# Attention, then a quantized convolution block: weight quantization spread over nine query blocks, a band split ahead of the last sums, stores on two queues

## The chip, the cores and the metric

The kernel runs on one core of a Trainium2 chip. A core has a matrix engine (TensorE, PE in the profile), a vector engine (VectorE, DVE), an activation engine (ScalarE, ACT), a general one (GpSimd, POOL) and a queue engine (SyncE, SP); 16 DMA engines move data between the memory of the chip and that of the core. Each engine works its own list of instructions in order, and they wait for one another by semaphores. The metric is the device time of one execution in microseconds, the median of several runs.

## The reference

Layer 0 is group norm, attention with four heads over 4096 positions, and a residual. Layer 1 quantizes the weights of two 3x3 convolutions to three bits and runs convolution, batch norm, Relu, convolution, batch norm, residual, Relu. x is (4, 128, 64, 64) in float32.

```python
# layer 0
x_norm = _group_norm(x, norm_w, norm_b)
qkv = jnp.einsum('oc,bchw->bohw', qkv_w, x_norm) + qkv_b[None, :, None, None]
q, k, v = (to_heads(t) for t in jnp.split(qkv, 3, axis=1))      # (b, 4, 4096, 32)
attn = jax.nn.softmax(jnp.einsum('bhid,bhjd->bhij', q, k) * scale, axis=-1)
out = jnp.einsum('bhij,bhjd->bhid', attn, v)                    # back to (b, c, h, w)
x = x + jnp.einsum('oc,bchw->bohw', proj_w, out) + proj_b[None, :, None, None]
# layer 1; lsq_quantize: round(clip(w / alpha_s, -4, 3)) * alpha_s
residual = x
out = conv3x3_decomposed(x, lsq_quantize(w1, alpha1))
out = relu(batchnorm(out, gamma1, beta1))
out = conv3x3_decomposed(out, lsq_quantize(w2, alpha2))
out = relu(batchnorm(out, gamma2, beta2) + residual)
```

## The kernel before

**Attention.** A block is one image `b` and one of its eight chunks of 512 queries, `qb`; the 32 blocks run in the order of `blocks`, and I write (b,qb) for one. A block has 32 steps `kt`, one for each 128 keys. In a step, `scores` multiplies keys and queries for four heads on PE (L435) and ACT takes the exponential into a tile `p` (L437); one step later at least, `weights` multiplies `p` with the values into `acc` (L448). The sums over the keys are kept apart: in most steps DVE adds `p` to `r` (L460), one add of 128x2048, and in the six steps of `MOVED` an accumulating DMA, issued by POOL, adds `p` to `rm` instead (L453, L455). The tiles `p` come from a pool of eight.

PE's order is written out by hand: three pairs of scores, one step of weights, three pairs, two steps of weights, and so on (the while loop). After each step of weights, `side(kt)` runs what `schedule` has put at that place: a list of (step, function), sorted, made anew for each block. So a function's place in it sets the place of its instructions on every engine's list at once.

**What follows a block** runs inside the next one (`finish_parts`): `merge` adds `rm` to `r`, `sums` has PE reduce `r` over partitions (L477), then ACT evacuates `ls`, `spread`, `invert` and `gather` bring the reciprocals round by DMA (`lq`, `rd`, `rc`, on SP), `weigh` multiplies `av` by `rc` on DVE (L526) two steps ahead of `project` on PE (`po`, L310), and `store` adds bias and residual `x` on DVE (L536) and writes `y` by POOL's queue (L537). `weigh` stands at step 25 to 27, `project` at 27 to 29. In qb 1 to 7 of the first three images the projections of the next image run along as well.

**Quantization.** `quant_tasks` makes eight generators: for each of the two weights one for the scalars (nine tiny DVE instructions) and three for three taps each (a load of 128x384 on SP, L172, and 13 DVE instructions of 128x384, L174 to L189, with tiles `tk` and `tq` from the pool `stage`). `pieces` strings them together: each `next(pieces)` runs up to the next `yield`. Before the change the last four instructions of a group have no `yield` behind them and run together with the load of the next group. `schedule` takes six pieces a block at steps 1, 6, 11, 16, 21, 26 of the blocks (3,1) to (3,6); they are used up in (3,5).

**Convolution.** The output of attention is read back from `y` in bands of 16 rows (four an image, `bandlist`), with a zero border by POOL memsets (L549 to L555). `split` parts a band into `hi` and `lo` on DVE (L562, L563), and PE takes 18 matmuls for a half band (L752). The tiles of bands come from the nine buffers that held keys. The first two bands are loaded and split inside the last block, and their convolutions run ahead of and between the last block's sums and projection. These lines set the order there:

```python
    conv(ready[0, 0, 0], early[0][:, 1, :], 1, wq[0])
    last["sums_at_once"]()
    load_band(*bandlist[2])
    conv(ready[0, 0, 1], early[1][:, 0, :], 0, wq[0])
    conv(ready[0, 0, 1], early[1][:, 1, :], 1, wq[0])
    last["project"]()
    last["store"]()
    split_band(*bandlist[2])
    last["bounds"]()
```

`layer` then goes through the bands: statistics on DVE (L816), a copy by ACT (L817), with loads three bands and splits two bands ahead (`first`). At the very end, for each of 16 quarters of an image (the first in two halves), DVE scales and adds the residual (L912), ACT applies Relu (L913), and SP issues the store of 512 KB (L914).

Of the kernel before, what the change touches and what calls it, by code (L numbers as in the profile page):

```python
# [78 lines left out]
def _fast_body(ctx, tc, x, norm_w, norm_b, qkv_wt, qkv_b, proj_wt, proj_b,  # L79
               w1, alpha1, gamma1, beta1, w2, alpha2, gamma2, beta2, out, cnt):  # L80
    nc = tc.nc
    B, C, H, W = x.shape
# [3 lines left out]
    NB = N // FB  # L86
    NK = N // P
# [53 lines left out]
    def quant_tasks(pool):  # L141

        tasks = []
        for i, (w, alpha) in enumerate(((w1, alpha1), (w2, alpha2))):
            al = const.tile([P, 1], F32, name=f"al{i}")
            nc.gpsimd.dma_start(out=al, in_=alpha.partition_broadcast(P))
            t = {n: const.tile([P, 1], F32, name=f"{n}{i}")
                 for n in ("ag", "a_s", "a_c", "a_h", "a_l", "inv", "ninv")}
            alpha_s.append(t["a_s"])


            def scalars(al=al, t=t):
                nc.vector.tensor_scalar(t["ag"], al, gfac, None, ALU.mult)
                nc.vector.tensor_tensor(t["a_s"], al, t["ag"], ALU.subtract)
                nc.vector.tensor_tensor(t["a_s"], t["ag"], t["a_s"], ALU.add)
                nc.vector.tensor_scalar(t["a_c"], t["a_s"], 4097.0, None, ALU.mult)
                nc.vector.tensor_tensor(t["a_h"], t["a_c"], t["a_s"], ALU.subtract)
                nc.vector.tensor_tensor(t["a_h"], t["a_c"], t["a_h"], ALU.subtract)
                nc.vector.tensor_tensor(t["a_l"], t["a_s"], t["a_h"], ALU.subtract)
                nc.vector.reciprocal(t["inv"], t["a_s"])  # L160
                nc.vector.tensor_scalar(t["ninv"], t["inv"], -1.0, None, ALU.mult)
                yield

            tasks.append(scalars)
            for c in range(3):


                def taps(i=i, c=c, w=w, t=t):
                    tk, tq = (pool.tile([P, 2, FB], F32, name=f"t{n}{i}{c}", tag=n) for n in "kq")
                    wr, q0, qh, ql = (u[:, e, : 3 * P].rearrange("p (t o) -> p t o", o=P)  # L170
                                      for u in (tk, tq) for e in range(2))
                    nc.sync.dma_start(out=wr, in_=w[:, 3 * c : 3 * c + 3, :])  # L172
                    yield
                    nc.vector.tensor_scalar(q0, wr, t["inv"], -8.0, ALU.mult, ALU.max)  # L174
                    nc.vector.tensor_scalar(q0, q0, 8.0, None, ALU.min)
                    nc.vector.tensor_scalar(qh, q0, SPLIT, None, ALU.add)
                    yield
                    nc.vector.tensor_scalar(qh, qh, SPLIT, None, ALU.subtract)
                    nc.vector.tensor_tensor(ql, q0, qh, ALU.subtract)
                    nc.vector.scalar_tensor_tensor(wr, qh, t["a_h"], wr, ALU.mult, ALU.subtract)  # L180
                    yield
                    nc.vector.scalar_tensor_tensor(wr, qh, t["a_l"], wr, ALU.mult, ALU.add)
                    nc.vector.scalar_tensor_tensor(wr, ql, t["a_h"], wr, ALU.mult, ALU.add)
                    nc.vector.scalar_tensor_tensor(wr, ql, t["a_l"], wr, ALU.mult, ALU.add)
                    yield
                    nc.vector.scalar_tensor_tensor(q0, wr, t["ninv"], q0, ALU.mult, ALU.add)
                    nc.vector.tensor_scalar(q0, q0, QN, QP, ALU.max, ALU.min)
                    nc.vector.tensor_scalar(q0, q0, ROUND, None, ALU.add)
                    nc.vector.tensor_scalar(wq[i][:, 3 * c : 3 * c + 3, :], q0, ROUND, None,  # L189
                                            ALU.subtract)  # L190

                tasks.append(taps)
        return tasks
# [350 lines left out]
    def band_tile(name):  # L544
        return stack_tile(name).rearrange("p (r w) -> p r w", w=PW)

    def border(t, g):

        nc.gpsimd.memset(f32(t)[:, :, 0:1], 0.0)  # L549
        nc.gpsimd.memset(f32(t)[:, :, W + 1 : W + 2], 0.0)  # L550
        r0, r1 = g * BR - 1, g * BR + BR + 1
        if r0 < 0:
            nc.gpsimd.memset(f32(t)[:, 0, 1 : 1 + W], 0.0)
        if r1 > H:
            nc.gpsimd.memset(f32(t)[:, BR + 1, 1 : 1 + W], 0.0)  # L555
        lo, hi = max(r0, 0), min(r1, H)
        return f32(t)[:, lo - r0 : hi - r0, 1 : 1 + W], lo, hi

    def split(t, name):

        hi, lo = band_tile(f"hi{name}"), band_tile(f"lo{name}")
        nc.vector.tensor_copy(hi, f32(t))  # L562
        nc.vector.tensor_tensor(lo, f32(t), f32(hi), ALU.subtract)  # L563
        return hi, lo
# [3 lines left out]
    def load_band(b, g):  # L568
        raw[b, g] = t = band_tile(f"t0_{b}_{g}")
        inner, lo, hi = border(t, g)  # L570
        nc.sync.dma_start(out=inner, in_=y0[b].rearrange("p (h w) -> p h w", w=W)[:, lo:hi, :])

    def split_band(b, g):
        ready[0, b, g] = split(raw[b, g], f"0_{b}_{g}")
# [3 lines left out]
    for j in range(NB):  # L578
        eng = (nc.sync, nc.scalar)[j % 2]
# [21 lines left out]
    def load_kv(b, j):  # L601
        load_k(b, j)
        load_v(b, j)
# [18 lines left out]
    def schedule(n, before):  # L622
        b, qb = blocks[n]
# [5 lines left out]
        def add(kt, f):  # L629
            todo.append((kt, f))  # L630
# [7 lines left out]
        if before:  # L638
# [3 lines left out]
            kt = kts[-1]  # L642
# [50 lines left out]
                    add(4 * j + 1, lambda j=j: load_kv(b + 1, j))  # L693
        if b > 0 and qb == 0:
            add(1, lambda: load_kv(b, NB - 1))
        if b == B - 1 and 0 < qb < NB - 1:
            for kt in range(1, NK - 1, 5):
                add(kt, lambda: next(pieces, None))
        if n == len(blocks) - 1:
            add(5, lambda: load_band(0, 0))  # L700
            add(13, lambda: split_band(0, 0))
            add(17, lambda: load_band(0, 1))
            add(24, lambda: split_band(0, 1))
        return sorted(todo, key=lambda t: t[0])

    pieces = (piece for task in quant_tasks(stage) for piece in task())
    steps = len(blocks) * NK
    at = {"pair": 0, "step": 0}
# [11 lines left out]
    def run_weights(count):  # L720
        for _ in range(min(count, steps - at["step"])):
            n, kt = divmod(at["step"], NK)
            if kt == 0:
                assert not todo
                todo[:] = schedule(n, parts.get(n - 1))
            weights(at["step"])
            at["step"] += 1
            if kt == NK - 2:
                parts[n] = finish_parts(n)
            if kt == NK - 1:  # L730
                parts[n]["copy"]()
            else:
                side(kt)
# [9 lines left out]
    bandlist = [(b, g) for b in range(B) for g in range(H // BR)]  # L743

    def conv(parts, ps, j, w):
        hi, lo = parts
        r0 = j * RB
        n = 0
        for part in (hi, lo):
            for tap in range(TAPS):  # L750
                kh, kw = divmod(tap, 3)
                nc.tensor.matmul(ps.rearrange("p (r w) -> p r w", w=W), w[:, tap, :],  # L752
                                 part[:, r0 + kh : r0 + kh + RB, kw : kw + W],
                                 start=(n == 0), stop=(n == 2 * TAPS - 1))
                n += 1
# [7 lines left out]
    conv(ready[0, 0, 0], early[0][:, 0, :], 0, wq[0])  # L763
    last["residual"]()
    conv(ready[0, 0, 0], early[0][:, 1, :], 1, wq[0])
    last["sums_at_once"]()
    load_band(*bandlist[2])
    conv(ready[0, 0, 1], early[1][:, 0, :], 0, wq[0])
    conv(ready[0, 0, 1], early[1][:, 1, :], 1, wq[0])
    last["project"]()  # L770
    last["store"]()
    split_band(*bandlist[2])
    last["bounds"]()
    att.close()

# [130 lines left out]
    for b in range(B):  # L906
        for j in range(4):
            for p in range(2 if b == j == 0 else 1):
                n = HN // 2 if b == j == 0 else HN
                y = res[b, j][:, p * n : (p + 1) * n]  # L910
                cs = slice(j * HN + p * n, j * HN + (p + 1) * n)
                nc.vector.scalar_tensor_tensor(y, cv[b][:, cs], a2, y, ALU.mult, ALU.add)  # L912
                nc.scalar.activation(y, y, AF.Relu, bias=c2)  # L913
                nc.sync.dma_start(out=out[b].rearrange("c h w -> c (h w)")[:, cs], in_=y)  # L914

# [456 lines left out]
```

## Time and profile before

| | us |
|---|---|
| median of 5 runs | 2574.32 |
| lowest and highest | 2571.59, 2575.25 |
| the profiled execution | 2572.48 |
| its span, first to last instruction | 2570.7 |
| PE busy | 2525.8 (98%) |
| DVE busy | 2138.8 (83%) |
| ACT busy | 2083.3 (81%) |
| adds of `r`, L460 | 768 of 2.289 |
| exponentials, L437 | 2048 of 1.033 |
| stores of the output, first to last issue | 2543.79 to 2563.49 |

The clock granted to PE was 0.995 on average. Times within the execution count from the start of the span. A row of the profile names line, engine, operation and tile, and says what ended the idle time before it; idle time of an engine that nobody waits for costs nothing. Attention takes the span up to 2255.8, the first convolution up to about 2397, the second up to 2542.

### The profile page before, as it was taken

How to read it: one execution, taken by the hardware profiler on the slowest of the kernel's cores; microseconds unless marked ns; L12 is line 12 of the kernel's file. 1: busy time of each engine (PE TensorE's matmuls, PEld its weight loads, DVE VectorE, ACT ScalarE, POOL GpSimd, SP SyncE). 2: the span in 40 equal slices, each digit the busy share in tenths (PEclk: the TensorE clock that was granted, in tenths of full speed). 3: DMA queues.
4: the chain of work that ended last, by engine and by line, in shares of the span. 5: the costliest groups of instructions: out<-in, count | busy, mean ns of one | idle time of the engine just before them, and what ended most of it. 6: DMA issues, size and time to landing. Idle time of an engine off the chain costs nothing.

```text
span 2570.7 us, 48634 instructions
## 1 busy us (share of the span) xinstructions
PE 2525.8 (98%) x20504; PEld 1231.9 (48%) x20504; DVE 2138.8 (83%) x1401; ACT 2083.3 (81%) x2278; POOL 280.0 (11%) x459
## 2 busy tenths in 40 slices
PE   9999999999999999999999999999999999999995
PEld 5444444444444444444444444444444444467774
DVE  6898888889988889889988888888999998854344
ACT  5888899998989899998988899999889899911224
POOL 2111111111011111110011111110000001000000
PEclk9999999999999999999999999999999999999998
DMA  6876766688767667697766666986755756635004
GB/s 186 193 189 171 172 157 163 161 197 192 166 142 187 169 157 169 156 215 174 167 171 159 162 158 151 205 203 142 159 117 133 164 125 139 148 79 162 1 1 165
DMA packets 147562, 400.06 MB, mean 156 GB/s; under 512 B 59256, under 2 KB 60024, under 8 KB 118792
## 3 DMA queue, kind: packets, MB, share of 16 engines
q0 software_dynamic: 45792, 280.33, 48.4%
q1 hardware_dynamic: 100824, 115.10, 16.9%
q8 instruction: 163, 2.67, 0.4%
q10 hardware_dynamic: 720, 1.44, 0.2%
q14 instruction: 63, 0.52, 0.1%
HBM read 105.32 MB, written 55.83 MB: 63 GB/s over the span
## 4 chain that ended last, share of the span: by engine, by line
PE 83%; DVE 10%; DMA 3%; issue 3%; ACT 1%; ACTq 0%; POOL 0%; SPq 0%; DVEq 0%; POOLq 0%
PE s L435 36%; PE acc L448 32%; PE c L752 9%; DVE r L460 7%; DMA rm<-p 3%; PE pq L310 1%; PE pk L310 1%; PE l L477 1%; PE po L310 1%; PE pv L310 1%; DVE res L912 1%; ACT p L437 0%; DVE r L458 0%; PE c_last L752 0%; DMA xh<-in_x_dram 0%
## 5 line engine op out<-in xcount | busy, mean ns | idle before, releaser
L437 ACT ACTIVATE p<-s 128x1024 f32<-128x1024 f32 x2048 | 1940.1, 1033 | 229.6 <-PE s L435 154.6
L460 DVE TENSOR_TENSOR r<-r,p 128x2048 f32<-128x2048 f32 x768 | 1758.3, 2289 | 93.6 <-ACT p L437 44.9
L435 PE MATMUL s<-q,k 64*128 64x512 f32 x8192 | 1159.7, 412 | 2.2 <-ACT p L437 1.6
L448 PE MATMUL acc<-p,v 128*32 128x512 f32 x8192 | 1021.1, 600 | 0.5 <-DVE v L364 0.5
L435 PEld LDWEIGHTS s<-q,k 64*128 64x128 f32 x8192 | 708.6, 185 | 631.4 <-issue 296.6
L448 PEld LDWEIGHTS acc<-p,v 128*32 128x32 f32 x8192 | 197.7, 108 | 452.0 <-issue 445.9
L455 POOL DMA_DIRECT2D rm<-p x160 | 138.5, 866 | 946.2 <-ACT p L437 837.7
L817 ACT COPY cv<-c 128x512 f32<-128x512 f32 x60 | 35.2, 587 | 201.9 <-DVE st L816 201.9
L752 PE MATMUL c<-hi,wq 128*128 128x512 f32 x540 | 139.2, 402 | 2.9 <-DVE hi L562 1.6
L752 PE MATMUL c<-lo,wq 128*128 128x512 f32 x540 | 138.6, 401 | 0.0
L816 DVE BATCH_NORM_STATS2 st<-c 128x6 f32<-128x512 f32 x60 | 41.9, 699 | 104.3 <-PE c L752 84.1
L752 PEld LDWEIGHTS c<-hi,wq 128*128 128x128 f32 x540 | 101.2, 188 | 32.5 <-DVE hi L562 2.5
L752 PEld LDWEIGHTS c<-lo,wq 128*128 128x128 f32 x540 | 101.6, 188 | 27.2
L458 DVE TENSOR_TENSOR r<-p,p 128x2048 f32<-128x2048 f32 x32 | 73.3, 2290 | 22.5 <-ACT p L437 22.5
L345 DVE SCALAR_TENSOR_TENSOR kst<-pk,b,kst 128x512 fp32r<-128x512 f32 x32 | 24.0, 751 | 72.1 <-ACT kst L344 72.1
L345 DVE SCALAR_TENSOR_TENSOR qst<-pq,b,qst 128x512 fp32r<-128x512 f32 x32 | 24.0, 750 | 41.2 <-ACT qst L344 41.1
L481 POOL DMA_DIRECT2D r<-rm x31 | 26.3, 848 | 162.0 <-PE s L435 95.7
L453 POOL DMA_DIRECT2D rm<-p x32 | 17.8, 556 | 230.7 <-ACT p L437 142.8
L349 POOL DMA_DIRECT2D qd<-qst x31 | 23.4, 754 | 177.6 <-DVE qst L345 160.7
L349 POOL DMA_DIRECT2D kd<-kst x28 | 20.6, 736 | 165.1 <-DVE kst L345 161.6
L477 PE MATMUL l<-r,ones 128*32 128x256 f32 (+1 forms) x504 | 37.9, 383 | 0.5 <-issue 0.5
L310 PE MATMUL po<-av,wp 128*32 128x512 f32 x256 | 33.4, 594 | 4.5 <-DVE av L526 4.5
(146 smaller groups left out, 724.8 us busy)
## 6 DMA issues: line engine op xcount, KB each, us to landing
rm<-p POOLq DMA_DIRECT2D x192, 1024.0 KB, 8.0
q<-qd SPq DMA_DIRECT2D x248, 128.0 KB
r<-rm POOLq DMA_DIRECT2D x31, 1024.0 KB, 7.6
x<-in_x_dram SPq DMA_DIRECT2D x80, 256.0 KB
k<-kd SPq DMA_DIRECT2D x124, 128.0 KB
qd<-qst POOLq DMA_DIRECT2D x31, 512.0 KB, 6.0
kd<-kst POOLq DMA_DIRECT2D x28, 512.0 KB, 3.8
y<-x POOLq DMA_DIRECT2D x32, 256.0 KB, 4.8
```

The lines of the kernel that those rows point to most:

```text
L310: nc.tensor.matmul(out[cs, :], w[:, cs], x, start=True, stop=True)
L345: nc.vector.scalar_tensor_tensor(lo, ps[what], bias, t[:, 0, :], ALU.add, ALU.subtract)
L349: (nc.sync if start else nc.gpsimd).dma_start(out=dst[b, j].rearrange("s p n -> p s n"), in_=t)
L435: nc.tensor.matmul(s[:, i, :], k[r, half, c0 : c0 + P], q[r, half, part, :], start=(part == 0), stop=(part == 1))
L437: nc.scalar.activation(pts[step][:, 2 * half : 2 * half + 2, :], s, AF.Exp, scale=SCALE)
L448: nc.tensor.matmul(acc[n][h * D : (h + 1) * D, :], v[:, kt % KB, h * D : (h + 1) * D], pt[:, h, :], start=(kt == 0), stop=(kt == NK - 1))
L455: nc.gpsimd.dma_start(out=msum[n], in_=pt, accum_op=ALU.add)
L458: nc.vector.tensor_tensor(rsum[n], pts[step - 1], pt, ALU.add)
L460: nc.vector.tensor_tensor(rsum[n], rsum[n], pt, ALU.add)
L477: nc.tensor.matmul(t["l"][h * D : (h + 1) * D, cs], ones, r[:, h, cs], start=first, stop=end)
L752: nc.tensor.matmul(ps.rearrange("p (r w) -> p r w", w=W), w[:, tap, :], part[:, r0 + kh : r0 + kh + RB, kw : kw + W], start=(n == 0), stop ...
L816: nc.vector.bn_stats(st[:, b * NB + c, :], ps[:, j, :])
```

## The change

The quantization of a group of taps gets one more `yield`, so that the load of the next group is a piece of its own: 32 pieces in place of 26 and a rest. They are taken from nine blocks: six in (1,0), five in (2,0), and three in each of (3,0) to (3,6). The cycle of scores and weights stays as it was. The third band is loaded at step 27 of the last block and split ahead of the last sums. Of the stores of the output, those of the second and fourth quarter of each image are issued by ACT.

```diff
                     nc.vector.tensor_scalar(wq[i][:, 3 * c : 3 * c + 3, :], q0, ROUND, None,
                                             ALU.subtract)
+                    yield
...
-        if b == B - 1 and 0 < qb < NB - 1:
-            for kt in range(1, NK - 1, 5):
+        if b == B - 1 and qb < NB - 1:
+            for kt in (1, 10, 20):
                 add(kt, lambda: next(pieces, None))
+        elif 0 < b and qb == 0:
+            for kt in (1, 10, 15, 20, 25) + ((29,) if b == 1 else ()):
+                add(kt, lambda: next(pieces))
         if n == len(blocks) - 1:
             add(5, lambda: load_band(0, 0))
             add(13, lambda: split_band(0, 0))
             add(17, lambda: load_band(0, 1))
             add(24, lambda: split_band(0, 1))
+            add(27, lambda: load_band(0, 2))
...
     conv(ready[0, 0, 0], early[0][:, 1, :], 1, wq[0])
+    split_band(*bandlist[2])
     last["sums_at_once"]()
-    load_band(*bandlist[2])
     conv(ready[0, 0, 1], early[1][:, 0, :], 0, wq[0])
     conv(ready[0, 0, 1], early[1][:, 1, :], 1, wq[0])
     last["project"]()
     last["store"]()
-    split_band(*bandlist[2])
     last["bounds"]()
...
                 nc.scalar.activation(y, y, AF.Relu, bias=c2)
-                nc.sync.dma_start(out=out[b].rearrange("c h w -> c (h w)")[:, cs], in_=y)
+                eng = nc.sync if j % 2 == 0 else nc.scalar
+                eng.dma_start(out=out[b].rearrange("c h w -> c (h w)")[:, cs], in_=y)
```

## The prediction

> **What bounds the kernel now.** I read the page's busy shares and its chain first, to learn which engine sets the pace:
>
> ```profile
> span 2570.7 us, 48634 instructions
> PE 2525.8 (98%) x20504; PEld 1231.9 (48%) x20504; DVE 2138.8 (83%) x1401; ACT 2083.3 (81%) x2278; POOL 280.0 (11%) x459
> PE 83%; DVE 10%; DMA 3%; issue 3%; ACT 1%; ACTq 0%; POOL 0%; SPq 0%; DVEq 0%; POOLq 0%
> ```
>
> The TensorE is busy 98% of the span, so nothing that leaves its instructions alone can win more than its idle time of 44.9 us, and 29 of that lie behind the last convolution. But 10% of the chain runs over DVE. The chain in order of time shows where: almost only DVE's adds `r` from 1818.99 to 2044.23, inside blocks (3,1) to (3,4). So next I asked what PE waited for, from the start of the last batch (1711) to the early convolution tiles (2330):
>
> ```profile
> PE po L310 <- DVE av L526: 4.5, 3, 2.5
> PE c L752 <- DVE hi L562: 1.6, 1, 1.6
> ```
>
> The columns are us in total, times, longest. Three times the output projection of a block stood in PE's queue before its input `av` was weighed by DVE. Once a convolution waited for the split of its band. The busy time of the engines block by block (stretch and length, then PE, PEld, DVE, ACT, POOL, clock, DMA) tells why:
>
> ```profile
> 1711.20:1780.70 69.50, 69.50 (x554) 29.48 (x554) 60.70 (x31) 62.78 (x70) 7.04 (x10) 1.00 0.72 161
> 1848.30:1917.20 68.90, 66.43 (x528) 27.89 (x528) 66.82 (x50) 60.10 (x67) 5.83 (x7) 1.00 0.56 125
> 1986.60:2055.20 68.60, 67.11 (x536) 28.78 (x532) 66.34 (x51) 60.20 (x67) 6.28 (x8) 1.00 0.69 150
> 2121.40:2190.90 69.50, 69.50 (x553) 29.48 (x554) 60.63 (x31) 62.79 (x69) 6.91 (x10) 1.00 0.69 145
> ```
>
> These are (3,0), (3,2), (3,4) and (3,6). In the first and last, without quantization, DVE has 8.8 us to spare and PE none. In the middle two DVE is down to 2.1 and 2.3 us and PE stands still for 2.5 and 1.5. Two microseconds are DVE's floor: adds that follow each other start 2.40 us apart though one lasts 2.29, and some 25 of these 0.1 us gaps stay in any block. Quantization saturates DVE there, and nothing else does.
>
> The end is bound otherwise. PE's last convolution ends near 2542; then come 17 scales, 17 Relus and 17 stores:
>
> ```profile
> 2542.25 19.35 DVE L912 SCALAR_TENSOR_TENSOR res<-cv,ba,res 128x512 f32<-128x512 f32 x17
> 2543.79 19.70 SPq L914 DMA_DIRECT2D out_dram<-res  x17
> 2544.90 17.89 ACT L913 ACTIVATE res<-res,bc 128x1024 f32<-128x1024 f32 x15 [0.47 <-DVE res L912]
> ```
>
> ```profile
> 2545.00:2550.00 5.00, 0.00 (x0) 0.00 (x0) 5.00 (x5) 4.81 (x5) 0.00 (x0) 0.63 0.72 283
> 2555.00:2560.00 5.00, 0.00 (x0) 0.00 (x0) 5.00 (x5) 4.79 (x5) 0.00 (x0) 0.50 1.01 404
> 2565.00:2571.00 6.00, 0.00 (x0) 0.00 (x0) 0.00 (x0) 0.00 (x0) 0.00 (x0) 0.50 0.34 133
> ```
>
> Here the last two columns matter: from 2550 the 16 DMA engines are full (share 1.01, 404 GB/s). The last Relu ends at 2562.79, and the data drain until about 2567.1.
>
> **What the Trainium skill says.** "DMA: Bandwidth & Descriptors", section "Issuing engines are not separate DMA queues": transfers issued by ScalarE and SyncE share the 16 engines, and several issuers save only sequencer time. The trace agrees: one queue alone already fills the engines, so a second has no bandwidth to add. "VectorE: DVE Perf Modes", section "Specifications": DVE runs at 0.96 GHz; its mode with one result a cycle would give 2048 / 0.96 = 2.13 us for an add (estimate), and the page's row shows 2.289. So the adds, and with them DVE's load, can't shrink by being moved. No page prices a wait inside a queue.
>
> **The change, part by part.**
>
> (a) Quantization leaves (3,1) to (3,5), where it is served six pieces a block. The pieces' prices, each from its first start to the start of DVE's next work in the saturated stretch: scalars 1.48 (1783.08 to 1784.56), and for a group of three taps A 1.12 (L174 to L176), B 1.39, C 1.84, D 1.71, in sum 6.06; with the added `yield` the weight load is a piece alone. Six groups and two scalars are 39.3 us of DVE work, unchanged in total. Now the last batch gets three pieces a block: at worst C, D and scalars in (3,1), 5.0 us, or B, C and D in (3,6), 4.9, against 8.8 - 2.2 = 6.6 free. The largest piece at step 20 makes the weighing at step 25 or 26 later by at most some 1.8 us, and in (3,0) and (3,6) `av` is ready 3.04 us before PE's `po` starts. So the three waits go: **-4.5 us**. Late next in these blocks is nothing of DVE: PE itself is the bound.
>
> (b) The first group goes to (1,0), the second to (2,0). (1,0) has 66.6 - 58.74 = 7.9 us of DVE idle and takes 7.5; (2,0) has 67.3 - 62.04 = 5.3 and takes 6.06. What counts is the lag at the weighing. A piece between two adds fills the 0.1 us gap as well, so it costs about 0.93, 1.2, 1.65, 1.5 (A: adds at 1802.01 and 1805.34 are 3.33 apart, less 2.40). In (2,0), A after step 10 to D after step 25 all stand ahead of the weighing, and DVE's idle stretches of 0.85, 0.71, 0.39 and 0.25 between, less 0.1 each, absorb: 0.93 - 0.75 + 1.2 - 0.61 + 1.65 - 0.29 + 1.5 - 0.15 = 3.5 us late. `av` ended at 1212.10 and PE began `po` at 1215.13, a reserve of 3.03: PE waits **+0.5** (ends 0 and 1.5). In (1,0), D comes behind the weighing: 0.93 - 0.37 + 1.2 - 0.15 - 0.86 + 1.65 = 2.4 late, against 660.87 - 658.20 = 2.67: 0. The lag carried into (1,1) and (2,1) is below 3 us and runs out there: of 69.8 and 66.5 us DVE works 65.0 and 62.4. The two 196 KB weight loads are one SP issue each (0.33 to 1.22), behind the K and V loads and ahead of `lq`, with at least five steps (some 10 us) before A: 0. They are moved, not added.
>
> (c) The third band. In the trace its load was issued at 2238.89, early enough; its border on POOL (2256.04) and its split on DVE (2276.87) were late. The split stood behind `store` (2276.21), though DVE was idle from 2259.8 to 2267.0, waiting for `ls`. Now load and border come at step 27: on SP ahead of the last residual load (one 0.36 us issue), on POOL ahead of the `rm` of step 28 and of one `y` store (two memsets, 0.3 us, while POOL waits for the previous `rm` to land at 2251.18). The split's 2.1 us fall into the 7 us hole and end by 2262, ahead of the reciprocals at 2267.04. PE starts the third tile at 2276.14 instead of 2277.70: **-1.55** (ends -1.6 and 0). DVE's bounds and statistics come 2 us earlier too, once `y` has landed (2279.57), so the fourth band's split (done by 2284) still precedes PE's need at 2284.8. Convolution runs without a gap from there to 2355, so the gain reaches the end.
>
> (d) Eight of the 17 stores go to ScalarE's queue. Each waits there for its own Relu and holds the next one back. ACT has some reserve: a Relu takes 1.145 us, but they start every 1.19, paced by DVE. With x for one issue and about 0.13 around it, the last Relu ends at 2544.90 + 15 x 1.145 + 7 (x + 0.13) = 2563.0 + 7x. Its own issue adds x, then about 0.55 to the first packet and 1.35 for 512 KB: the tail moves by 8x - 2.2 against 2567.1. In the trace SP needs 0.34 for such a store; at the kernel's start ACT needs 0.42 to 0.46 where SP needs 0.39 to 0.43 for the same loads. With x = 0.36 to 0.45 the tail loses 0.7 to 1.4; I take **+1.0** (ends -0.5, if the early hole in the transfers at 2546 closes, and +3, at ACT's 0.66 of 20.4 to 22.4).
>
> Sum: -4.5 + 0.5 - 1.55 + 1.0 = **-4.55 us**. The profiled execution took 2572.48, 1.84 below the median of 2574.32; off the median this gives **2569.8**. A measurement of this kernel can tell about 0.2% (5.15 us) from no change: the forecast, -0.18%, lies just inside.
>
> **The rivals.**
>
> *The gains hold and the costs hide.* No wait in (2,0) and a tail at +0.3 or better: -4.5 - 1.55 + 0.3 = -5.75, 2568.6; with the tail 0.5 shorter, 2567.8. For it: the reserve in (2,0) is missed by only 0.5. Against it: at the end ACT is 96% busy, and seven issues must fit somewhere.
>
> *ScalarE's queue becomes the bound.* The place is the last 28 us, the price x. Break-even with the other parts' -5.55 is 8x = 7.75, x = 0.97; slower by over 0.2% begins at x = 1.6. For it: SP's third store took 0.87, and single SP issues reach 1.9 when earlier ones are being worked off; on ACT such a wait stops the Relus. Against it: ACT's own seven issues are 0.42 to 0.66, and with a slower producer less is queued. At x = 1.8: +12.2 - 5.55, 2581.0.
>
> *The overload only moves.* If (1,0) and (2,0) stall PE as (3,2) did, 2.5 each: -4.5 + 5 - 1.55 + 1 = 0, 2574.3. For it: both would have DVE as full as the middle blocks. Against it: they start without lag, and the lag stops growing.
>
> *The early split does nothing*, because a buffer or the border comes late: +1.55, 2571.4. Against it: the load's buffer was free at 2238.89.
>
> **How the numbers follow.** The forecast 0.45 (2568.9 to 2572), costs that hide 0.35, moved overload or a useless split 0.10, ACT's queue 0.10, of which three parts in ten stay within 0.2%. Part of the forecast's own spread crosses the bound, so I put faster at 0.37, same at 0.56, slower at 0.07. The range, 2566.5 to 2575, takes in all but the far end of ACT's queue and a baseline that wanders by over a microsecond.
>
> **What would show it.** Right: no wait of `po` on `av` in the last batch, some 0.5 us in (2,0); no wait of the third tile for `hi`; Relu pairs about 2.8 us apart at the end. Wrong: a wait of `po` over 1.5 us in (1,0) or (2,0), new PE waits on DVE in (1,1) or (2,1), ACT issues over 1 us, or a span end that moves without these.

## The result and the profile after

The changed kernel takes 2568.95 us in the median of 29 runs (2565.66 to 2572.17), the kernel before 2573.21 in 49 runs; the ratio is 0.9983, 95% interval 0.9977 to 0.9988. The forecast was 2569.8, or 4.55 us less than before; it is 4.3 less. The profiled execution took 2566.82.

The page's span, busy shares and chain by engine, as shown of before:

```profile
span 2565.0 us, 48629 instructions
PE 2524.5 (98%) x20504; PEld 1232.2 (48%) x20504; DVE 2138.7 (83%) x1401; ACT 2083.3 (81%) x2278; POOL 280.6 (11%) x459
PE 89%; DMA 4%; issue 3%; DVE 3%; ACT 1%; POOL 0%; SPq 0%; ACTq 0%; POOLq 0%; DVEq 0%
```

No engine does more or less than before: all busy times are the same within 1.3 us. Only DVE's part of the chain fell, from 10% to 3%, and PE's rose. The change rearranged waits and removed no work.

PE's waits between 595 and 2330, that is from the second image to the early convolution tiles:

```profile
PE s L436 <- ACT p L438: 2.3, 3, 1.0
PE po L311 <- DVE av L527: 0.8, 2, 0.6
PE acc L449 <- DVE x L537: 0.5, 1, 0.5
```

In the same stretch before, `po` waited 4.5 us, the third tile 1.6 for `hi`, and `s` had this line:

```profile
PE s L435 <- ACT p L437: 1.4, 3, 0.9
```

The 4.5 us of `po` are down to 0.8: 0.6 in (2,0), and 0.2 late in the last image. The wait of the third tile for `hi` is gone. There is a new line, `acc` waiting for `x`, and `s` waits 0.9 us longer for `p`. The engines block by block, for (3,0), (3,2), (3,4), (3,6), then (1,0), (1,1) and (2,0), with the columns that the prediction used:

```profile
1712.80:1782.30 69.50, 69.50 (x552) 29.49 (x552) 62.95 (x37) 62.74 (x69) 7.00 (x10) 1.00 0.72 163
1849.20:1915.40 66.20, 66.20 (x528) 27.96 (x528) 60.90 (x37) 60.05 (x67) 6.19 (x8) 1.00 0.57 126
1984.90:2051.70 66.80, 66.80 (x536) 28.84 (x532) 61.61 (x39) 60.08 (x66) 6.19 (x8) 1.00 0.64 139
2118.00:2187.40 69.40, 69.40 (x552) 29.42 (x552) 64.04 (x41) 62.73 (x69) 6.37 (x9) 1.00 0.69 145
598.70:665.40 66.70, 66.28 (x528) 27.95 (x528) 61.93 (x51) 60.15 (x67) 5.63 (x7) 1.00 0.75 170
665.40:735.50 70.10, 69.59 (x556) 30.29 (x556) 67.89 (x50) 63.08 (x69) 7.38 (x10) 1.00 0.71 166
1157.00:1224.70 67.70, 67.08 (x536) 28.76 (x532) 65.52 (x45) 60.23 (x66) 6.20 (x8) 1.00 0.78 176
```

In the last image PE now fills its stretch to the last digit, and DVE keeps 5 us and more. (1,1) and (2,0) have become the tight ones: DVE is down to 2.2 us of idle time in each, about what (3,2) had before, and PE loses 0.5 and 0.6. The instructions in (2,0), DVE first, then PE:

```profile
1212.08 0.61 DVE L186 SCALAR_TENSOR_TENSOR tk<-tk,ninv 128x384 f32<-128x384 f32 x1
...
1213.79 2.29 DVE L461 TENSOR_TENSOR r<-r,p 128x2048 f32<-128x2048 f32 x1
1215.99 0.68 DVE L527 TENSOR_TENSOR av<-av,rc 128x512 f32<-128x512 f32 x1
```

```profile
1216.73 1.06 PE L311 MATMUL po<-av,wp 128*32 128x512 f32 x8 [0.62 <-DVE av L527]
```

The last piece of the group (L186 on) stands ahead of the weighing of `av`, and `po` waits for that: 0.62 us.

The end, first as a timeline, then the last columns of the windows for the transfers:

```profile
2538.80 19.96 SPq L921 DMA_DIRECT2D out_dram<-res  x9
...
2541.10 0.37 ACTq L921 DMA_DIRECT2D out_dram<-res  x1
2541.51 2.19 ACT L919 ACTIVATE res<-res,bc 128x1024 f32<-128x1024 f32 x2 [0.44 <-DVE res L918]
2543.73 0.35 ACTq L921 DMA_DIRECT2D out_dram<-res  x1
2544.13 2.19 ACT L919 ACTIVATE res<-res,bc 128x1024 f32<-128x1024 f32 x2 [0.43 <-ACT res L919]
2546.35 0.34 ACTq L921 DMA_DIRECT2D out_dram<-res  x1
```

```profile
2550.00:2555.00 5.00, 0.00 (x0) 0.00 (x0) 5.00 (x5) 4.11 (x5) 0.00 (x0) 0.50 1.00 403
```

A pair of Relus and its store on ACT recur every 2.62 us (2541.51, 2544.13); two quarters of an image, 2 x 512 KB, need 2.59 at 404 GB/s (an estimate from the rate of before). The DMA engines stay full, at 403 GB/s with two queues where one gave 404.

### The profile page after: what moved, and what is told of

Read it like the earlier page. It is cut to its first block, busy times and chain, and to the rows that moved or that the text cites. A ratio compares the mean times of both kernels' runs of the same rounds, so it can differ in the third digit from the quotient of the medians.

```text
span 2565.0 us, 48629 instructions
## 1 busy us (share of the span) xinstructions
PE 2524.5 (98%) x20504; PEld 1232.2 (48%) x20504; DVE 2138.7 (83%) x1401; ACT 2083.3 (81%) x2278; POOL 280.6 (11%) x459
## 3 DMA queue, kind: packets, MB, share of 16 engines
q8 instruction: 163, 2.67, 0.4%
## 4 chain that ended last, share of the span: by engine, by line
PE 89%; DMA 4%; issue 3%; DVE 3%; ACT 1%; POOL 0%; SPq 0%; ACTq 0%; POOLq 0%; DVEq 0%
PE s L436 40%; PE acc L449 35%; PE c L759 9%; DMA rm<-p 3%; DVE r L461 2%; PE l L478 1%; PE po L311 1%; PE pk L311 1%; PE pq L311 1%; PE pv L311 1%; ACT p L438 1%; DMA t<-y 1%; ACT res L919 0%; PE c_last L759 0%; DMA xh<-in_x_dram 0%
## 5 line engine op out<-in xcount | busy, mean ns | idle before, releaser
L345 ACT ACTIVATE kst<-pk,b 128x512 fp32r<-128x512 f32 x32 | 22.3, 701 | 16.5 <-PE pk L311 16.5
```

## The experiments

All edits are to the kernel before unless said otherwise. The marks in the table are the starts of ACT's copies of `acc` at the end of each block and, for the tail, the start of `bc`, the last constant of the second batch norm, 0.3 us ahead of the first scale of `res`. So each column is one stage of one profiled execution, in us.

| kernel | image 1 | image 2 | (3,0) to (3,6) | last copy to `bc` | tail: `bc` to the end of the span |
|---|---|---|---|---|---|
| before | 557.0 | 555.4 | 479.7 | 286.2 | 28.7 |
| changed | 558.4 | 555.8 | 474.6 | 284.6 | 28.0 |
| changed, once more | 558.0 | 555.8 | 474.8 | 284.6 | 28.0 |
| quantization alone | 559.2 | 555.5 | 474.7 | 286.2 | 28.6 |
| band alone | 557.7 | 554.9 | 479.8 | 284.6 | 28.1 |
| split alone | 557.7 | 555.6 | 481.4 | 284.6 | 28.1 |
| stores alone | 556.6 | 555.0 | 481.9 | 286.2 | 28.5 |
| all stores on ACT | 557.8 | 555.0 | 481.1 | 286.2 | 31.5 |
| light taps, places of before | 556.5 | 555.0 | 475.2 | 286.2 | 28.1 |
| light taps, places of the change | 556.8 | 554.7 | 474.7 | 284.6 | 28.1 |
| changed, retimed | 558.3 | 554.4 | 475.6 | 284.6 | 28.0 |
| changed, all in the last image | 557.0 | 555.6 | 475.5 | 284.6 | 28.5 |
| the same, stores on SP | 557.6 | 554.9 | 474.7 | 284.6 | 28.2 |

Each part shows in its own column; image 0 took 598.5 to 600.8 without order, and that alone is a good part of the scatter of whole times.

**Quantization alone.** The `yield` and the new places of the pieces.

```diff
+                    yield
...
-        if b == B - 1 and 0 < qb < NB - 1:
-            for kt in range(1, NK - 1, 5):
+        if b == B - 1 and qb < NB - 1:
+            for kt in (1, 10, 20):
                 add(kt, lambda: next(pieces, None))
+        elif 0 < b and qb == 0:
+            for kt in (1, 10, 15, 20, 25) + ((29,) if b == 1 else ()):
+                add(kt, lambda: next(pieces))
```

> The change's quantization schedule alone, band and stores as before. If the saturated DVE of the last image was the cause, the three waits of po on av (4.5 us in the trace) go and one of about 0.6 us appears in (2,0), with about 0.5 us at the start of (1,1): 3 to 4 us faster than before, ratio about 0.9987. Rival, that the work only moves its wait to (1,0) and (2,0): within 1 us of before, with waits of po on av of 2 us or more there. Rival, that most of the gain came from the stores: within 1 us of before, without such waits.

Measured: ratio 0.9995, interval 0.9987 to 1.0004, so less than I expected, and by the times alone not told from no change. The medians are 1.4 us apart. PE's waits from 595 to 2330:

```profile
PE s L436 <- ACT p L438: 3.1, 3, 1.1
PE po L311 <- DVE av L527: 0.6, 1, 0.6
PE acc L449 <- DVE x L537: 0.5, 1, 0.5
```

The three waits of `po` are gone and the two new ones are there. The last image is 5.0 us shorter, but image 1 is 2.2 longer, more than the 0.5 and a little that I had put there: a wait of `s` on ACT's `p`, 1.1 us at 799 near the end of (1,2), is not in the trace of before. The stages add up to about -2.7.

**Band alone.**

```diff
+            add(27, lambda: load_band(0, 2))
...
+    split_band(*bandlist[2])
     last["sums_at_once"]()
-    load_band(*bandlist[2])
...
-    split_band(*bandlist[2])
     last["bounds"]()
```

> The early load and split of the third band alone. If the wait of the third tile for its hi was the whole effect, the 1.56 us gap goes, the rest of the trace stays, and the time falls by 1.5 us (ratio 0.9994). Rival, that the split makes something else late (the reciprocals of the last block, or the y store through POOL): within 0.5 us of before, with a new wait between 2255 and 2300.

Measured: ratio 0.9989, interval 0.9981 to 0.9998, which holds the expected 0.9994; the medians are 2.4 us apart, so whole times alone do not divide the gain between this part and the quantization. The stage falls by 1.6, as expected; no new wait stands between 2255 and 2300. PE's waits from 1711 to 2330 of this kernel show the two causes apart, those of `av` as before and `hi` absent:

```profile
PE po L310 <- DVE av L526: 4.6, 4, 2.4
PE s L435 <- ACT p L437: 0.2, 1, 0.2
```

**Split alone.**

```diff
+    load_band(*bandlist[2])
+    split_band(*bandlist[2])
     last["sums_at_once"]()
-    load_band(*bandlist[2])
...
-    split_band(*bandlist[2])
     last["bounds"]()
```

> The kernel before with the third band's load and split both right ahead of the last sums (no load at step 27). If only the split's place on DVE counted, the 1.56 us gap of the third tile is gone just as with the early load, and from the end of the last block to the first scale of the tail it takes 284.6 us, not 286.2. Rival, that the load must be early: a gap of some 1 to 4 us at the third tile, and hi of that band waiting for the load.

Measured: 2572.75 in one run; the stage is 284.6. DVE's timeline of this kernel has the split in the hole ahead of the reciprocals:

```profile
2262.32 0.77 DVE L562 CAST hi<-t 128x1188 fp32r<-128x1188 f32 x1
2263.12 1.40 DVE L563 TENSOR_TENSOR lo<-t,hi 128x1188 fp32r<-128x1188 f32 x1
2269.67 0.95 DVE L499 RECIPROCAL rc<-ls 128x128 f32<-128x128 f32 x1 [5.15 <-ACT ls L485]
```

The stage is as short as with the early load. So this part's gain is the split's place on DVE; no gain of the early load shows.

**Stores alone, and all stores on ACT.**

```diff
-                nc.sync.dma_start(out=..., in_=y)
+                eng = nc.sync if j % 2 == 0 else nc.scalar
+                eng.dma_start(out=..., in_=y)
```

> Two queues for the stores alone. My forecast was a tail longer by 1.0 us (from the first scale of the tail to the end of the span). The trace of the changed kernel says about 0 to -0.7: an issue on ACT takes 0.34, an undelayed Relu starts every 1.06, so a pair of quarters takes 2.62 against 2.59 that the transfers need. Theory now: the transfers stay the bound, difference 0 within 0.5 us. Rival, that the second queue itself shortens the end: faster by 0.7 us or more, with the last data coming earlier after the first scale than 25.8 us.

Measured: ratio 1.0000, interval 0.9992 to 1.0009. The tail is 28.5; kernels with all stores on SP show 28.1 to 28.7, those with two queues 28.0 to 28.5. Neither the 1.0 us loss that I forecast nor a gain is there.

For the other, every store is `nc.scalar.dma_start`.

> All 17 stores issued by ACT, which doubles the suspected cost. If ACT's issues delay its Relus by 0.42 each, a quarter takes 1.06 + 0.42 = 1.48 us against 1.30 for its transfer, so ACT becomes the bound: 15 x 1.48 from the first full quarter, the last Relu 22 us after it instead of 17.9, and the tail 2 to 3 us longer than with SP alone (ratio about 1.001). Rival, that a second queue or ACT's queue is as good as SP's whatever ACT does: no difference, or faster.

Measured: ratio 1.0010, interval 1.0004 to 1.0017, slower by 2.6 us (2.1 between the medians); the tail is 2.7 longer than before's. Its timeline, with ACT's Relus and stores in turn:

```profile
2548.55 1.15 ACT L913 ACTIVATE res<-res,bc 128x1024 f32<-128x1024 f32 x1 [0.42 <-ACT res L913]
2549.72 0.34 ACTq L914 DMA_DIRECT2D out_dram<-res  x1
2550.11 1.15 ACT L913 ACTIVATE res<-res,bc 128x1024 f32<-128x1024 f32 x1 [0.42 <-DVE res L912]
```

A quarter recurs every 1.56 us, above the 1.30 of its transfer (512 KB at 404 GB/s, an estimate): ACT is the bound. The mechanism of the rival exists, then; with half the stores it stands just at the point where it decides (2.62 against 2.59). That an issue on ACT holds back the next Relu by about 0.42 is shown; with 1.15 of a Relu that waits, not my 1.06, the period is 1.56.

**Light taps.** In both kernels the 13 DVE instructions of a group are one, which leaves out the rounding and clipping of the weights:

```diff
-                    ... (the 13 instructions)
+                    nc.vector.tensor_scalar(wq[i][:, 3 * c : 3 * c + 3, :], wr, t["inv"], None,
+                                            ALU.mult)
```

First with the places of before:

> The kernel before with the 13 DVE instructions of a group of taps cut to one that scales the loaded weights, so that the weights are not rounded or clipped; the loads and the scalars stay. If all that the last image loses comes from DVE's quantization, (3,0) to (3,6) take 474.6 us, not 479.7 to 481.9, as in the changed kernel, and no wait of po on av is left. Rival, that something else than DVE's quantization slowed these blocks (the weight loads on SP, DMA): 477 us or more.

Measured: 475.2, and 2567.09 for the one run. PE's waits from 1711 to 2330:

```profile
PE c L740 <- DVE hi L550: 1.6, 1, 1.6
PE s L423 <- ACT p L425: 0.2, 1, 0.2
```

The waits of `po` are gone with the work, while its loads are in place. So what the last image lost was DVE's quantization, and the changed kernel, at 474.6, has recovered all of it.

**Changed, retimed.**

```diff
-            for kt in (1, 10, 15, 20, 25) + ((29,) if b == 1 else ()):
+            for kt in (1, 4, 8, 13, 18, 23) if b == 1 else (1, 6, 11, 16, 28):
```

> The changed kernel with other steps in two blocks: (1,0) takes its six pieces at 1, 4, 8, 13, 18, 23 in place of 1, 10, 15, 20, 25, 29, and (2,0) its five at 1, 6, 11, 16, 28 in place of 1, 10, 15, 20, 25. By the lag reckoned from the trace of before, the weighing is 2.1 us late in (1,0) against a reserve of 2.67 and 2.3 in (2,0) against 3.03, and the store of (1,0) is no longer held up by the last piece. If lag at these two places is the cause, the wait of po in (2,0) (0.6) and that of acc for x at the start of (1,1) (0.5) both go: 1.1 us faster than the changed kernel. Rival, that the sum of DVE work in the block decides and not its place: both waits stay or turn up elsewhere in (1,0) to (2,1), no gain.

Measured: ratio to before 0.9974, interval 0.9963 to 0.9985. Both waits are gone; from 595 to 1300 PE has only this left:

```profile
PE s L436 <- ACT p L438: 1.4, 2, 1.2
```

(2,0) of this kernel:

```profile
1156.90:1223.80 66.90, 66.90 (x536) 28.89 (x532) 64.69 (x44) 60.30 (x67) 6.20 (x8) 1.00 0.80 179
```

DVE has 2.2 us of idle time there, as in the changed kernel, but PE loses nothing. So it was the pieces' places, not their sum, that cost the 1.1 us. Whole times don't show it: this interval overlaps that of the changed kernel. The wait of 1.2 at 796 is still there.

**All in the last image, without and with stores on SP.** Both start from the changed kernel.

```diff
-            for kt in (1, 10, 20):
+            for kt in (1, 7, 13, 19, 28):
                 add(kt, lambda: next(pieces, None))
-        elif 0 < b and qb == 0:
-            for kt in (1, 10, 15, 20, 25) + ((29,) if b == 1 else ()):
-                add(kt, lambda: next(pieces))
```

> The changed kernel with all quantization in the last image: five pieces a block at steps 1, 7, 13, 19, 28 of (3,0) to (3,6), none in (1,0) and (2,0). 39.3 us over seven blocks are 5.6 each, below the 6.6 that DVE has free, and the weighing is late by at most 0.9 us where 1.06 is the reserve. If the place of the pieces decides, (3,0) to (3,6) take 474.7 us as in the changed kernel, images 1 and 2 go back to the 557 and 555.2 of before, and the time is 1 to 2 us below the changed kernel (ratio to before 0.9977). Rival, that five pieces a block in a row saturate DVE as six did: waits of po on av of 1 us and more in (3,1) to (3,5), and no gain on the changed kernel.

Measured: ratio 0.9971, interval 0.9959 to 0.9983. (3,2) and (3,5) of this kernel:

```profile
1849.90:1916.40 66.50, 66.50 (x532) 28.07 (x530) 64.21 (x44) 60.38 (x66) 5.61 (x7) 1.00 0.65 141
2052.80:2119.00 66.20, 66.20 (x530) 27.91 (x528) 63.92 (x44) 60.08 (x66) 5.69 (x8) 1.00 0.65 139
```

DVE is down to 2.3 us idle, about as in (3,2) before, and yet PE waits for nothing. The kernel before had two such blocks as well, (3,3) and (3,5), with 2.2 us idle and PE full:

```profile
1917.20:1986.60 69.40, 69.40 (x552) 29.41 (x550) 67.21 (x56) 62.70 (x68) 6.76 (x9) 1.00 0.62 141
2055.20:2121.40 66.20, 66.20 (x528) 27.97 (x528) 63.98 (x42) 60.06 (x66) 5.64 (x8) 1.00 0.57 126
```

Little idle time on DVE does not cost by itself; it costs when the weighing is later than its reserve allows. With light taps and the places of before, the weighing in (3,2) ended 59.0 us after the start of the block, and PE began `po` 2.67 later: that is the reserve. In the kernel before it ended after 64.3, so 5.2 late, and here after 59.6, 0.6 late. Four of the five pieces lie ahead of the weighing, one of them a load without DVE work, and the fifth behind, at step 28. Number and places of the pieces changed together in this experiment; that the places alone can decide is shown by the retimed kernel.

The next two ran on the same chip:

> All quantization in the last image (five pieces a block at 1, 7, 13, 19, 28), the early split, and all stores on SP again. If the second queue gives nothing, as the tails of 28.1 to 28.7 us on one queue and 28.0 to 28.5 on two say, this is as fast as with two queues: ratio 0.9971 within 0.001, tail 28 to 28.7, and 1 to 3 us below the changed kernel. Rival, that the second queue helps after all: 0.7 us or more slower than with it, a tail of 29.

> The changed kernel once more, on one chip with the next: ratio about 0.9983, with the waits of 0.6 us of po in (2,0) and 0.5 us of acc for x at the start of (1,1).

Measured: 0.9971 (0.9960 to 0.9983) with stores on SP against 0.9981 (0.9975 to 0.9988) for the changed kernel, medians 2566.0 and 2569.26. This version leaves the stores on SP and has the lowest median of all. The intervals of the ratios overlap a little; compared directly, the mean of its 7 runs is 2.9 us below that of the 21 runs of the changed kernel, 95% interval 1.3 to 4.5. The waits of 0.6 and 0.5 and the one in (1,2) are absent from its trace.

**Light taps with the places of the change** ask for the cause of the wait in (1,2), which in the changed kernel reads:

```profile
795.64 0.73 PE L436 MATMUL s<-q,k 64*128 64x512 f32 x4 [0.92 <-ACT p L438]
```

The chain of work leads from there to an accumulating transfer of a tile `p`, the fourth of the block:

```profile
779.73 14.73 DMA rm<-p
```

> The changed kernel with the 13 DVE instructions of a group of taps cut to one that scales the loaded weights (no rounding, no clipping); loads and places as in the changed kernel. It asks where the wait of 0.9 to 1.2 us at 795 comes from, near the end of (1,2), which three kernels with pieces in (1,0) show and which is 0 to 0.4 without: there the fourth accumulation into rm lands 14.7 to 15.0 us after its issue, not 13.8 to 14.0. If DVE's work in (1,0) is the cause, 13.9 us here and no wait over 0.5. If the weight load on SP, which moves the later transfers by one place in the queue's order, is the cause: 14.7 or more and the wait as before.

Measured, in one run: the fourth accumulation lands after 14.0 us and the wait is 0.2.

```profile
rm<-p POOLq DMA_DIRECT2D x1, 1024.0 KB, 14.0
```

So DVE's work in (1,0), not the load, brings the wait about, as far as one run can show it. How that reaches a transfer in (1,2), some 110 us later, stays open: DVE had caught up by about 740, and this transfer and that of `kd` just before it are issued at the same place in the block, within 0.02 us, in all thirteen kernels. The transfer of `kd` is slower in the same four kernels too: 10.1 to 10.4 us to landing against 9.2 to 9.6 in the others.

## Why the prediction was right, point by point

**(a) The last image, -4.5.** Right: -5.1 in the profile, and the waits went as named. The five kernels of the old schedule take 479.7 to 481.9 in that stage, and before is the shortest of them; against their mean, 480.8, the gain is 6.2. So the 4.5 us, which were the waits of one trace, were somewhat low. Light taps show that DVE's quantization was the whole of it.

**(b) (1,0) and (2,0), +0.5.** The wait in (2,0) came at its place with 0.62, and the lag of 3.5 us that I reckoned by hand was 3.4: from the start of the block (1155.8 before, 1157.0 after) the weighing of `av` ended after 56.3 us before and 59.7 after, against a reserve of 3.03. In (1,0) the weighing was 2.5 late against my 2.4 and a reserve of 2.67, and `po` did not wait. What failed is the rest of "(1,0): 0". I had followed the last piece, behind the weighing, only into (1,1)'s slack and not to the next instruction on DVE that PE waits for: `store` took its turn at 666.64, and the first step of weights in (1,1) needs the buffer that it frees, since `acc` and `po` share a pool of two buffers:

```profile
664.43 2.29 DVE L461 TENSOR_TENSOR r<-r,p 128x2048 f32<-128x2048 f32 x1
666.64 0.75 DVE L537 SCALAR_TENSOR_TENSOR x<-po,bp,x 128x512 f32<-128x512 f32 x1
```

```profile
667.44 1.07 PE L449 MATMUL acc<-p,v 128*32 128x512 f32 x8 [0.51 <-DVE x L537]
```

A new wait of PE on DVE in (1,1) was one of the signs that I had named for being wrong, and it came. The lag took nearly all of (1,1) to run out: DVE worked 67.9 of 70.1 us in (1,1), where it had worked 65.0 of 69.8. Retiming removed the wait. With the one in (1,2), about 0.9, which I had not foreseen at all, images 1 and 2 lost 1.8 us instead of 0.5 in the profiled execution. Other kernels agree: image 1 takes 558.0 to 559.2 with pieces in (1,0) at full work, and 556.5 to 557.8 without.

**(c) The third band, -1.55.** Right: -1.6, and the third tile starts at 2272.71, 1.00 us after the last `po` at 2271.71, with no wait. That the load was early enough before, as its issue at 2238.89 said, is shown by the split alone.

**(d) The stores, +1.0.** Wrong in size: 0 within the scatter, and the Relu pairs came every 2.62 us, not 2.8. Two terms of the sum were too large. An undelayed Relu starts 1.06 us after the one before (2541.51 and 2542.57), since the two overlap; I had taken 1.145 from the row. And an issue with what lies around it holds back a Relu by 0.42, not by the 0.49 of x = 0.36 and 0.13. Over seven pairs that is 7 x 0.085 + 7 x 0.07 = 1.1 us: the last Relu ended 22.2 us after the first scale, where my sum with x = 0.36 gives 23.3. The 1.0 that I took stood for x = 0.4, and the trace has 0.34 to 0.37. With both put right (22.2, an issue of 0.34, and the 0.55 and 1.35 of the prediction) the data of the last store would be out 24.4 us after the first scale if ACT alone decided. The transfers of before needed 24.9, so they stay the bound. What "DMA: Bandwidth & Descriptors" of the Trainium skill says in the section "Issuing engines are not separate DMA queues", that transfers run on the same 16 engines whichever engine issues them, is borne out: 403 GB/s on two queues, 404 on one.

The errors nearly cancelled: +1.3 in (b), -1.0 in (d), -0.6 in (a). That the total is nearer to the forecast than its parts is luck. The forecast's baseline, a median of 5 runs, was also 1.1 us above that of the 49. Of the rivals, the costs that hide were half right: the stores cost nothing, but (2,0) did wait. The overload that only moves is refuted in its size (2.5 each) and right in kind (0.6 and 0.5). ACT's queue needs all stores on it to appear; the reading that single issues of SP reach 1.9 us was too low, since in the trace of before one load of `x` took 8.4 (at 2229.71), but no store on ACT took over 0.37. And the early split that does nothing is refuted by the 1.6 us.

## What to carry to other kernels

When an engine off the critical path is near saturation, don't price a move by the sum of its work in a block. Follow its lag, that is how much later than before it comes to each instruction that another engine waits for, with gaps and pieces in order, and compare it with the reserve, the time by which that instruction used to be early. Do this for the instructions behind the moved piece too. Here a block with some 2 us of idle time on DVE cost PE 2.5 us, 0.6 or nothing, and what decided was the lag at the weighing. And a second queue gave nothing where the DMA engines were full already (403 and 404 GB/s), while each store issued by ACT held the next Relu back by about 0.42 us, which has to fit into the reserve of that engine.

## What the runs showed that I had not expected

Relus of 1.15 us that are ready back to back start every 1.06. And with six pieces of quantization in (1,0), one accumulating transfer two blocks later took 14.7 to 15.0 us to land, in all four such kernels; it took 13.8 to 14.3 in the nine without that work. The link between them was not found.
